# Layer 1 of a two-layer graph transformer: the squares of the first normalization a chunk behind their sums, and the turn of h behind the products of the next to last formed pair

## The chip, the core and the metric

The kernel runs on one core of one Trainium2 chip. A core has five engines that each work through a queue of their own, in order, and wait for one another at semaphores: TensorE (PE in the profile; its weight loads are PEld), VectorE (DVE), ScalarE (ACT), GpSimd (POOL) and SyncE (SP, which here only issues DMAs). POOL issues the indirect DMAs, too: gathers that fetch listed rows, and puts that store rows at listed places. The metric is the device time of one execution in microseconds, and the kernel before takes 1840.38 us in the median of three runs.

## The reference

Two layers of the same form follow each other on 2708 tokens of width 512, with 8 heads of 64 and a hidden width of 2048. Each token attends to the tokens that a sparse 0/1 matrix names (its own included), and then passes a feed-forward part. Everything is float32.

```python
q, k, v = (h @ Wq.T + bq), (h @ Wk.T + bk), (h @ Wv.T + bv)        # 8 heads of 64
scores = where(mask == 0, -1e9, einsum('nhd,mhd->hnm', q, k) / 8)
ctx = einsum('hnm,mhd->nhd', softmax(scores), v).reshape(n, 512)
h1 = layer_norm(h + ctx @ Wo.T + bo, ln1_g, ln1_b)                 # the first normalization
h2 = layer_norm(h1 + relu(h1 @ W1.T + b1) @ W2.T + b2, ln2_g, ln2_b)
```

## The kernel before, in words

**Work by edges.** Attention is done over the listed neighbours alone. The 2708 tokens are sorted by their number of neighbours into 22 tiles of 128 (the last has 20), and each tile has a fixed number of places for neighbours. Two places make a *step*: POOL gathers the two rows of keys and values (`kv`, L1119, one gather a place), DVE multiplies the keys by the queries (L1156), adds up the scores (L1162), and, for a step begun three steps earlier, weights the first row of values (L1192) and adds both to the sum (L1199). ACT takes the exponentials of a step begun two steps earlier (`p`, L1175) and weights its second row of values, a head at a time (L1182, eight instructions). When a tile's steps are over, DVE makes the sums of its weights (L1207 to L1222) and ACT divides (`cx`, L1230, eight instructions). A gather reuses the place of an earlier step's rows, and so waits for that step's L1199.

**Blocks and chunks.** The projections, normalizations and the feed-forward part are done for blocks of two tiles (256 tokens), numbered k = 0 to 10 here. The feed-forward part of a block runs over 16 chunks f of 128 hidden units: PE makes the chunk's hidden values (`pf`, L1601 or L1785, four products), ACT adds a bias and cuts at zero (`ft`, L1796 in the formed blocks). In blocks 0, 1 and 10, two more products for each chunk add to the block's output (`second`, L1574), three chunks behind. In layer 1's blocks 2 to 9, the *formed* blocks (`feed_forward_by_seven`), two chunks make a pair, and the eight products of a pair are replaced by seven half-width ones (`products(j)`, L1774) on sums that DVE forms (`sums(j)`, L1751 to L1754); the last pair is done plainly (L1805, L1809) between `products(5)` and `products(6)`.

**What runs beside a block.** While block k is in its feed-forward part, the next block is made ready by the generator `attended`: PE turns `cx` (`tp`, L1354; the copy back is ACT's `cT`, L1359) and multiplies by Wo (`o`, L626); DVE adds the residual and makes the sum over the row in one instruction (`total`, L1312, `h<-o,xb`; the negated mean `nm` follows, L1323); ACT makes the sum of squares (`squares`, L1329); POOL makes the reciprocal root from it (`centred`, `va` L1336 and `rd` L1338) and DVE subtracts the mean and multiplies by the gain (L1339); ACT scales (`scaled`, L1345, `h<-h,rd`). Then PE turns `h` (`turned`: eight `tp<-ident,h`) and ACT copies it to `hT` (L1359, eight instructions), which all 16 chunks of the next block read. `hT` has one buffer. The block before, k-1, is finished by the generator `ended` (the *tail*): squares, centred, scaled, then POOL adds the shift by an accumulating DMA (L1348, `h<-ln_b`) and puts the rows to the output (L1082, `out<-h`). An `h` buffer (four of them) is written again by `total` two blocks later, once its put has landed.

**What sets the order.** The order is written out by hand for all five engines: the loop at the end of `by_edges` walks over the chunks of each block, and at each chunk takes the next piece of `attended`, of the tail and of the attention. The tail's pieces go by the table `TAILS` (the first entry up to block 2, the second for later blocks); attention goes by credits in the tables `PACES` (block 0), `PACE` and `PACE7` (the formed blocks), which `advance` turns into whole steps. In layer 1 the pieces of `attended` stand at chunks 10 to 13, the turn at chunk 15 ahead of that chunk's `advance`. Each `yield` in a generator is a place where the loop puts in other work; what stands behind a waiting instruction on its engine waits with it.

Of the kernel before, what the change touches and what calls it, by code (L numbers as in the profile page):

```python
# [25 lines left out]
NFC = FF // P  # L26
# [29 lines left out]
    (0.0,) * 4 + (0.6,) + (1.3,) * 4 + (0.6,) * 2 + (0.0,) * 2 + (0.5, 0.8, 2.4),  # L56
    (0.0,) * 4 + (0.4, 1.1, 0.3, 1.1, 0.3, 1.0, 1.0, 1.5, 0.4, 0.9, 0.0, 2.2),
)
TAILS = ((1, 2, 4, 5, 8), (5, 7, 8, 9, 10))
FORMED = (1, 1)  # L60
FORMS = (3, 5, 7, 9, 11, 13, 15)
PACE = (
# [425 lines left out]
def by_edges(ctx: ExitStack, tc: tile.TileContext, x, xT, adj, layers, out, redo):  # L488
# [874 lines left out]
    class Layer:  # L1363
# [132 lines left out]
        def attended(self, block, got, xbs=None, soon=False):  # L1496

            cTs, hs, norms = [], [], []

            def turn(g):  # L1500
                r = size(g)
                cx = got.pop(g)
                cT = dn.tile([P, NC, P], F32, tag="cT", name="cT", bufs=3)
                flip(cx, r, cT[:, :, :r], self.bv)
                cTs.append((g, r, cT))

            turn(block[0])
            xbs = xbs or self.residuals(block)
            yield
            if block == blocks[0]:  # L1510
                turn(block[1])
                yield
            for i, xb in enumerate(xbs):
                g, r, cT = cTs[i]
                o = project(lambda c: cT[:, c, :r], r, self.wo, "o")
                h = dn.tile([P, DM], F32, tag="h", name="h", bufs=4)
                if self.n == 0 or soon:
                    nc.vector.tensor_tensor(h[:r], o[:r], xb[:r], ALU.add)
                    plus_rest(h[:r], o, r)
                    if self.n == 0:  # L1520
                        nc.vector.tensor_tensor(h[:r], h[:r], self.bo[:r], ALU.add)
                    norm(h, r, self.g1, None if soon else self.e1b2)
                else:
                    last = xb[:r]
                    parts = [o[:r]] + rest(o, r)
                    for part in parts[:-1]:
                        nc.vector.tensor_tensor(h[:r], part, last, ALU.add)
                        last = h[:r]
                    norms.append(Norm(h, r, self.g1, xb).total(parts[-1], last))
                hs.append(h)  # L1530
                if len(cTs) == 1:
                    turn(block[1])
                for one in norms[-1:]:
                    one.squares()
                yield
            if norms:
                for one in norms:
                    one.centred()
                yield
                for one in norms:  # L1540
                    one.scaled()
            yield hs
# [10 lines left out]
        def feed_forward(self, block, hs, hT):  # L1553
# [70 lines left out]
            if apart:  # L1624
                for f in range(4):
                    second(f, block[1], slice(0, DM // 2))
                quarters(NFC - 1)
            for g in () if apart else block:
                for f in range(NFC - LAG, NFC):
                    second(f, g)  # L1630
                    if g == block[-1] and f == NFC - LAG:
                        quarters(NFC - 1)
# [106 lines left out]
        def feed_forward_by_seven(self, k, block, hs, hT):  # L1739
# [41 lines left out]
            for f in range(NFC):  # L1781
                j = f // 2
                pf = ps_f.tile([P, DM], F32, tag="f", name="pf")
                for c in range(NC):
                    nc.tensor.matmul(  # L1785
                        pf[:, :W],
                        self.w1[j][:, c, f % 2 * P : f % 2 * P + P],
                        hT[:, c, :],
                        start=(c == 0),
                        stop=(c == NC - 1),  # L1790
                    )
                if f % 6 < 4:
                    ft = dn.tile([P, W], F32, tag="ft", name="ft", bufs=4)
                else:
                    ft = self.more_fts[f % 2]
                nc.scalar.activation(ft, pf[:, :W], AF.Relu, bias=self.b1[:, f : f + 1])  # L1796
                fts.append(ft)
                if f % 2 == 0 and j > 0:
                    sums(j - 1)
                yield None  # L1800
                if f % 2 and j > 1:
                    products(j - 2)
            for i in range(2):
                f, w = 2 * J + i, self.w2[J]
                nc.tensor.matmul(a0, fts[f][:, :P], w[:, i, :], start=False, stop=False)  # L1805
# [248 lines left out]
    for n in range(NL):  # L2054
# [48 lines left out]
        for k, block in enumerate(blocks):  # L2103
# [12 lines left out]
            else:  # L2116
                working = now.feed_forward(block, hs, hT)
            for f, zs in enumerate(working):
                if f == NFC:
                    break  # L2120
                if n > 0 and f == 2:
                    for g, h in zip(block, hs):
                        added_row(h, size(g), now.e1b2)
# [11 lines left out]
                if more and f == 11 + 2 * (k + n == 0):  # L2135
                    until(blocks[k + 1][1])
                    next(projecting)
                if more and n > 0 and f in (12, 13):
                    next(projecting)
                if more and n == 0 and f == 12 + 2 * (k == 0):  # L2140
                    *_, hs_next = projecting
                if more and f == NFC - 1:
                    finish(asking)
                    hT = now.turned(blocks[k + 1], hs_next)
                advance((PACE7 if seven else PACE if k else PACES)[n][f])
                if more and n > 0 and f == 13:
                    *_, hs_next = projecting
                if f in (0, 3, 7, 9) and (f or k):
                    next(asking, None)
                if k == 0 and len(now.w1) < NFC // 2 and f % 2 == 0:  # L2150
# [132 lines left out]
```

## Time and profile before

| | us |
|---|---|
| three runs: median (lowest to highest) | 1840.38 (1840.02 to 1844.04) |
| the profiled execution's own time | 1839.64 |
| its span, first to last instruction | 1837.4 |
| PE busy in the span | 1793.4 (98%) |
| DVE busy | 1484.5 (81%) |
| ACT busy | 1000.9 (54%) |
| POOL busy | 852.1 (46%) |

Layer 1's feed-forward part begins at 1142.79 us of the span (block 0) and its last block at 1791.80 us. Starts and lengths are in microseconds from the first instruction; in a waits row the columns are the waiting engine, its tile and line, what it waited for, then the total, the number of waits and the longest. In a timeline row they are start, length, engine, line, operation, what it writes and reads, and the number of instructions merged into the row; the bracket at the end is the idle time ahead of it and what ended it. A windows row gives a stretch, its length, and for each engine the busy time in it, then the granted clock of TensorE as a share. Ends of matmuls are modelled, so starts are the safer reading. An engine's idle time is put down to what came last before it ended.

### The profile page before, as it was taken

Reading aid. Unit: us, or ns where it says so; the run is one execution under the profiler, and the core shown is the slowest. Engines: PE = TensorE matmul, PEld = TensorE weight load, DVE = VectorE, ACT = ScalarE, POOL = GpSimd, SP = SyncE. Lnnn points to the kernel's source line nnn. Section 1 sums busy time; section 2 is a strip of 40 time slices with the busy share of each in tenths; the row PEclk is TensorE's granted clock in tenths of the full one; section 3 lists DMA queues with packets and bytes.
Section 4 is the critical chain, followed back from the end, with each engine's and each line's share of the span. In section 5 each row is a group of like instructions: output and inputs, shape, how many; then the busy total and the mean of one; then the engine's idle time right before and its main releaser. Section 6 shows DMA issues by size and latency. Waiting matters only on the chain. (4 is left out here: it accounts for less than half of the span.)

```text
span 1837.4 us, 24293 instructions
## 1 busy us (share of the span) xinstructions
PE 1793.4 (98%) x6931; PEld 1233.9 (67%) x6931; DVE 1484.5 (81%) x2667; ACT 1000.9 (54%) x3399; POOL 852.1 (46%) x830
## 2 busy tenths in 40 slices
PE   9999999999999999999999999999999999999997
PEld 4444456567776867777777545666887788778776
DVE  5986778988989888899885277888988989889953
ACT  4770445554556546475553114677665767577641
POOL 3234755544445544454430133466555555555512
PEclk9999999999999999999999999999999999999999
DMA  9997987756676666666652877967787887876731
GB/s 342 374 338 257 371 279 238 243 177 222 209 240 229 205 218 205 224 231 187 222 185 83 301 279 255 318 193 280 235 256 227 278 256 218 275 222 191 225 86 35
DMA packets 192777, 432.26 MB, mean 235 GB/s; under 512 B 21222, under 2 KB 89946, under 8 KB 192632
## 3 DMA queue, kind: packets, MB, share of 16 engines
q0 software_dynamic: 76992, 264.49, 44.3%
q1 hardware_dynamic: 105482, 144.51, 23.1%
q10 hardware_dynamic: 10158, 21.61, 3.1%
q8 instruction: 57, 0.93, 0.2%
q14 instruction: 88, 0.72, 0.1%
HBM read 362.63 MB, written 57.11 MB: 228 GB/s over the span
## 5 line engine op out<-in xcount | busy, mean ns | idle before, releaser
L1119 POOL DMA_INDIRECT kv<-kv_d,listed x420 | 521.1, 1241 | 442.1 <-DVE acc L1199 172.5
L1785 PE MATMUL pf<-hT,w 128*128 128x256 f32 x2048 | 467.1, 380 | 9.1 <-ACT ft L1796 9.1
L1785 PEld LDWEIGHTS pf<-hT,w 128*128 128x128 f32 x2048 | 387.6, 190 | 75.2 <-ACT ft L1796 12.2
L1182 ACT ACTIVATE kv<-kv,p 128x64 f32<-128x64 f32 x1232 | 311.0, 334 | 5.0
L1156 DVE TENSOR_TENSOR kv<-kv,q 128x1024 f32<-128x1024 f32 (+1 forms) x222 | 256.9, 1157 | 17.3 <-DMA q<-q_d,ident_i 10.8
L1162 DVE TENSOR_REDUCE sc<-kv 128x16 f32<-128x1024 f32 (+1 forms) x222 | 258.0, 1162 | 7.6
L1199 DVE TENSOR_TENSOR acc<-acc,kv 128x1024 f32<-128x1024 f32 (+2 forms) x178 | 205.5, 1155 | 37.1 <-ACT kv L1182 23.1
L1796 ACT ACTIVATE ft<-pf,b 128x256 f32<-128x256 f32 x192 | 88.7, 466 | 232.8 <-PE pf L1785 218.2
L1175 ACT ACTIVATE p<-sc,listed 128x8 f32<-128x8 f32 x420 | 103.4, 295 | 106.9 <-DVE sc L1162 85.4
L1601 PEld LDWEIGHTS pf<-hT,w 128*128 128x128 f32 x768 | 130.2, 190 | 39.4 <-issue 24.9
L1601 PE MATMUL pf<-hT,w 128*128 128x256 f32 (+1 forms) x768 | 155.1, 350 | 0.1
L626 PE MATMUL o<-wo,cT 128*128 128x512 f32 x336 | 151.2, 594 | 2.5 <-ACT cT L1359 1.8
L1286 POOL TENSOR_TENSOR rd<-va,mhalf 128x1 f32<-128x1 f32 (+1 forms) x48 | 43.8, 912 | 224.7 <-DVE va L1284 224.2
L1574 PE MATMUL a<-w,ft 128*128 128x512 f32 x288 | 135.1, 593 | 0.0
L1192 DVE TENSOR_TENSOR kv<-kv,p 128x512 f32<-128x512 f32 (+1 forms) x178 | 123.8, 695 | 3.4 <-ACT p L1175 3.2
L626 PEld LDWEIGHTS o<-wo,cT 128*128 128x128 f32 x336 | 63.2, 190 | 70.8 <-issue 60.1
L751 DVE MAX8 tops<-code 128x8 f32<-128x247 f32 (+2 forms) x242 | 78.6, 400 | 27.2 <-ACT code L746 27.0
L1230 ACT ACTIVATE cx<-acc,su 128x64 f32<-128x64 f32 (+1 forms) x352 | 88.3, 335 | 14.4 <-DVE su L1222 11.9
L1182 ACT ACTIVATE acc<-kv,p 128x64 f32<-128x64 f32 (+1 forms) x352 | 88.8, 334 | 1.4
L1774 PE MATMUL a<-w,forms 128*128 128x256 f32 x288 | 85.7, 379 | 0.0
L1774 PE MATMUL c<-w,forms 128*128 128x256 f32 x288 | 85.7, 379 | 0.0
L746 ACT ACTIVATE code<-aj 128x1354 bf16<-128x1354 int32 (+1 forms) x44 | 73.4, 1722 | 20.5 <-POOL aj L740 16.6
(258 smaller groups left out, 2820.3 us busy)
## 6 DMA issues: line engine op xcount, KB each, us to landing
forms<-form_d SPq DMA_DIRECT2D x336, 128.0 KB
aj<-in_adj SPq DMA_DIRECT2D x42, 677.0 KB
kv_d<-kvs ACTq DMA_DIRECT2D x21, 512.0 KB
h<-ln_b POOLq DMA_DIRECT2D x41, 256.0 KB
xg<-in_xT SPq DMA_DIRECT2D x19, 512.0 KB
w<-in_W SPq DMA_DIRECT2D x16, 512.0 KB
kv<-kv_d,listed POOLq DMA_INDIRECT x420
zT_d<-zT SPq DMA_DIRECT2D x22, 256.0 KB
```

The lines of the kernel that those rows point to most:

```text
L626: nc.tensor.matmul(o[:r], xs(c), wm[:, c, :], start=(c == 0), stop=(c == NC - 1))
L1119: return nc.gpsimd.indirect_dma_start(out=to, out_offset=None, in_=table[:, :], in_offset=bass.IndirectOffsetOnAxis(ap=s, axis=0), bounds_ ...
L1156: nc.vector.tensor_tensor(kv[:r, :c, :DM], kv[:r, :c, :DM], self.q[:r].unsqueeze(1).to_broadcast([r, c, DM]), ALU.mult,)
L1162: nc.vector.tensor_reduce(self.sc[:r, s0 : s0 + c, :], kv[:r, :c, :DM].rearrange("p s (h d) -> p s h d", d=DK), AX.X, ALU.add,)
L1175: nc.scalar.activation(p[:r, s, :], self.sc[:r, s, :], AF.Exp, bias=minus[:r, g, s : s + 1])
L1182: nc.scalar.activation(to[:, i, hd], kv[:r, i, DM + h * DK : DM + (h + 1) * DK], AF.Copy, scale=p[:r, s0 + i, h : h + 1],)
L1192: nc.vector.tensor_tensor(to[:, 0, :].rearrange("p (h d) -> p h d", d=DK), kv[:r, 0, DM:].rearrange("p (h d) -> p h d", d=DK), p[:r, s0, : ...
L1199: nc.vector.tensor_tensor(self.acc[:r, :c, :], self.acc[:r, :c, :], kv[:r, :c, DM:], ALU.add)
L1574: nc.tensor.matmul(a[:r, cols], fts[f][:, c0 : c0 + r], self.w2[f // 2][:, f % 2, cols], start=(f == 0), stop=(f == NFC - 1),)
L1601: nc.tensor.matmul(pf[:, :w], self.w1[f // 2][:, c, f % 2 * P : f % 2 * P + P], hT[:, c, :w], start=(c == 0), stop=(c == NC - 1),)
L1774: nc.tensor.matmul(to, left, right, start=start, stop=stop)
L1785: nc.tensor.matmul(pf[:, :W], self.w1[j][:, c, f % 2 * P : f % 2 * P + P], hT[:, c, :], start=(c == 0), stop=(c == NC - 1),)
```

## The change

Five places change, all of them in the order of layer 1; the instructions are the same ones.

1. In `attended`, the squares of a tile are issued one chunk behind its `total`, so at chunks 12 and 13 instead of 11 and 12; `centred` moves to chunk 14 and `scaled` to chunk 15.
2. The loop turns `h` where the generator of the feed-forward part yields once more, behind its 16 chunks: in the formed blocks this stands behind `products(5)`, ahead of the last pair; in blocks 0 and 1 behind the last products of the block's first tile.
3. Chunk 15's `advance`, which stood behind the turn, now stands ahead of it.
4. The second entry of `TAILS` is one lower throughout: the tails from block 3 on are issued a chunk earlier.
5. The end of the loop is told by a list of outputs instead of by the chunk's number.

```diff
-TAILS = ((1, 2, 4, 5, 8), (5, 7, 8, 9, 10))
+TAILS = ((1, 2, 4, 5, 8), (4, 6, 7, 8, 9))
...
             for i, xb in enumerate(xbs):
+                for one in norms:
+                    one.squares()
                 g, r, cT = cTs[i]
...
-                for one in norms[-1:]:
-                    one.squares()
                 yield
             if norms:
+                norms[-1].squares()
+                yield
                 for one in norms:
                     one.centred()
                 yield
...
             for g in () if apart else block:
+                if self.n == NL - 1 and g == block[-1]:
+                    yield None
                 for f in range(NFC - LAG, NFC):
                     second(f, g)
...
                 if f % 2 and j > 1:
                     products(j - 2)
+            if self.n == NL - 1:
+                yield None
             for i in range(2):
...
             for f, zs in enumerate(working):
+                if zs:
+                    break
                 if f == NFC:
-                    break
+                    hT = now.turned(blocks[k + 1], hs_next)
+                    continue
...
-                if more and n > 0 and f in (12, 13):
+                if more and n > 0 and f in (12, 13, 14):
                     next(projecting)
+                if more and n > 0 and f == NFC - 1:
+                    *_, hs_next = projecting
...
                 if more and f == NFC - 1:
                     finish(asking)
-                    hT = now.turned(blocks[k + 1], hs_next)
+                    if n == 0:
+                        hT = now.turned(blocks[k + 1], hs_next)
                 advance((PACE7 if seven else PACE if k else PACES)[n][f])
-                if more and n > 0 and f == 13:
-                    *_, hs_next = projecting
```

**The end of block 5, PE.** Before, the turn of `h` follows the products of chunks 14 and 15 (`pf`):

```order
L1785 MATMUL pf<-hT,w_8330 128x256 x8
L1354 MATMUL tp<-ident,h 128x128 x8
L1774 MATMUL a_11896<-forms 128x256
L1774 MATMUL c_11818<-forms 128x256
L1774 MATMUL c_11819<-forms 128x256
L1774 MATMUL c_11818<-w_8305,forms 128x256
L1774 MATMUL a_11895<-w_8305,forms 128x256
L1774 MATMUL c_11819<-w_8305,forms 128x256
L1774 MATMUL a_11895<-w_8305,forms 128x256
L1805 MATMUL a_11895<-w_8920,ft 128x512 x2
```

Now:

```order
L1789 MATMUL pf<-hT,w_8330 128x256 x8
L1778 MATMUL a_11896<-forms 128x256
L1778 MATMUL c_11818<-forms 128x256
L1778 MATMUL c_11819<-forms 128x256
L1778 MATMUL c_11818<-w_8305,forms 128x256
L1778 MATMUL a_11895<-w_8305,forms 128x256
L1778 MATMUL c_11819<-w_8305,forms 128x256
L1778 MATMUL a_11895<-w_8305,forms 128x256
L1354 MATMUL tp<-ident,h 128x128 x8
L1811 MATMUL a_11895<-w_8920,ft 128x512 x2
```

The turn has moved behind the seven products of pair 5; the last pair (L1805, L1809) and `products(6)` are what is left between it and the next block.

**The end of block 5, ACT.** Before, `u` (L1827) is the copy of a sum of the block that has just ended:

```order
L1345 ACTIVATE h<-h,rd 128x512 x2
L1796 ACTIVATE ft<-pf,b_8175 128x256 x2
L1359 ACTIVATE hT<-tp,ln_b 128x128 x8
L1175 ACTIVATE p<-sc,listed 128x8 x2
L1182 ACTIVATE kv<-kv,p 128x64 x8
L1230 ACTIVATE cx<-acc,su 128x64 x8
L1175 ACTIVATE p<-sc,listed 128x8 x2
L1182 ACTIVATE kv<-kv,p 128x64 x8
L1827 COPY u_12385<-c_11818 128x256
```

Now:

```order
L1800 ACTIVATE ft<-pf,b_8175 128x256 x2
L1345 ACTIVATE h<-h,rd 128x512 x2
L1175 ACTIVATE p<-sc,listed 128x8 x2
L1182 ACTIVATE kv<-kv,p 128x64 x8
L1230 ACTIVATE cx<-acc,su 128x64 x8
L1175 ACTIVATE p<-sc,listed 128x8 x2
L1182 ACTIVATE kv<-kv,p 128x64 x8
L1359 ACTIVATE hT<-tp,ln_b 128x128 x8
L1833 COPY u_12385<-c_11818 128x256
```

The scaling stands behind both evictions of `ft`, and the attention of chunk 15 (two steps, and here the division of a tile) stands between the scaling and the copies to `hT`.

**The end of block 7, DVE**, from the second tile's `total` on. Before:

```order
L1312 ISA h,zsum<-o,xb 128x512
L1312 ISA zsum 128x1
L1323 TENSOR_SCALAR nm<-zsum 128x1
L1339 SCALAR_TENSOR_TENSOR h<-h,nm,ln_g 128x512 x2
L1156 TENSOR_TENSOR kv<-kv,q 128x2x512
L1162 TENSOR_REDUCE sc<-kv 128x16
L1192 TENSOR_TENSOR kv<-kv,p 128x512
L1199 TENSOR_TENSOR acc<-acc,kv 128x1024
L1751 TENSOR_TENSOR forms<-ft 128x128
L1752 TENSOR_TENSOR ft<-ft 128x128
```

Now:

```order
L1312 ISA h,zsum<-o,xb 128x512
L1312 ISA zsum 128x1
L1323 TENSOR_SCALAR nm<-zsum 128x1
L1156 TENSOR_TENSOR kv<-kv,q 128x2x512
L1162 TENSOR_REDUCE sc<-kv 128x16
L1192 TENSOR_TENSOR kv<-kv,p 128x512
L1199 TENSOR_TENSOR acc<-acc,kv 128x1024
L1755 TENSOR_TENSOR forms<-ft 128x128
L1756 TENSOR_TENSOR ft<-ft 128x128
L1757 TENSOR_TENSOR forms<-forms,ft 128x128
L1758 TENSOR_TENSOR forms<-ft,forms 128x128
L1339 SCALAR_TENSOR_TENSOR h<-h,nm,ln_g 128x512 x2
```

A step of attention and the four sums of a pair have moved ahead of `centred` (L1339).

**Block 5, POOL**, from the shift for the block's own residual (the first `h<-ln_b`) to the tail's put. Before:

```order
L1348 DMA h<-ln_b 128x512 x2
L1119 DMA kv<-kv_d_112,listed 128x1024 x4
L1336 TENSOR_SCALAR va<-sq 128x1
L1338 TENSOR_TENSOR rd<-va,mhalf 128x1
L1336 TENSOR_SCALAR va<-sq 128x1
L1338 TENSOR_TENSOR rd<-va,mhalf 128x1
L1119 DMA kv<-kv_d_112,listed 128x1024 x2
L1348 DMA h<-ln_b 128x512 x2
L1119 DMA kv<-kv_d_112,listed 128x1024 x2
L1082 DMA out<-h,ident_i 2708x512 x2
```

Now:

```order
L1348 DMA h<-ln_b 128x512 x2
L1119 DMA kv<-kv_d_112,listed 128x1024 x2
L1336 TENSOR_SCALAR va<-sq 128x1
L1338 TENSOR_TENSOR rd<-va,mhalf 128x1
L1336 TENSOR_SCALAR va<-sq 128x1
L1338 TENSOR_TENSOR rd<-va,mhalf 128x1
L1119 DMA kv<-kv_d_112,listed 128x1024 x4
L1348 DMA h<-ln_b 128x512 x2
L1082 DMA out<-h,ident_i 2708x512 x2
```

The tail's roots stand two gathers earlier; the tail's shift (the second `h<-ln_b`) still has six gathers between it and the first, and the put follows it at once. In blocks 6, 7 and 8 this number stays what it was (five, six and eight); in blocks 3 and 4 it falls from seven to five and from eight to six.

## The prediction

> **What bounds the kernel now.** The page comes first:
>
> ```profile
> PE 1793.4 (98%) x6931; PEld 1233.9 (67%) x6931; DVE 1484.5 (81%) x2667; ACT 1000.9 (54%) x3399; POOL 852.1 (46%) x830
> ```
>
> TensorE has 44 us of idle time in the whole span, so a reordering can win little, and everything it can win lies in PE's waits. Those stand in the view of waits, asked for PE and ACT:
>
> ```profile
> PE tp L1354 <- ACT h L1345: 9.4, 8, 2.4
> PE pf L1785 <- ACT ft L1796: 9.1, 7, 2.6
> ACT xb L1329 <- DVE nm L1323: 48.9, 13, 6.9
> ```
>
> The first row is the turn waiting for the scaled `h` (9.4 us in 8 waits). The second is PE waiting for an eviction of the formed blocks; the third says why ACT is late there: it stands at the squares, waiting for DVE's mean, with `ft` queued behind. These two are what the change is aimed at. Where they fall is read from the windows, one for each block of layer 1, from the block's first `pf` to the next block's (columns: PE, PEld, DVE, ACT, POOL busy, granted clock, DMA share, GB/s); the last row is a short piece behind the turn in block 6:
>
> ```profile
> 1214.16:1277.87 63.71, 63.71 (x225) 41.13 (x224) 56.07 (x76) 49.43 (x183) 44.44 (x41) 1.00 0.82 277
> ...
> 1339.30:1405.62 66.32, 61.77 (x271) 49.60 (x270) 58.52 (x100) 42.50 (x153) 36.34 (x35) 1.00 0.75 236
> 1405.62:1472.08 66.46, 63.09 (x272) 50.67 (x271) 59.25 (x99) 44.77 (x162) 35.67 (x35) 0.97 0.82 258
> 1472.08:1535.11 63.03, 61.69 (x271) 49.60 (x270) 57.00 (x96) 44.82 (x161) 34.88 (x34) 1.00 0.81 251
> 1535.11:1600.40 65.29, 62.88 (x271) 50.94 (x270) 58.63 (x101) 40.95 (x144) 40.88 (x39) 0.97 0.81 246
> 1600.40:1665.47 65.07, 61.75 (x272) 49.61 (x271) 56.30 (x92) 44.49 (x161) 34.19 (x31) 1.00 0.68 211
> 1665.47:1728.55 63.08, 61.52 (x271) 49.60 (x270) 58.16 (x104) 44.48 (x161) 38.87 (x36) 1.00 0.78 243
> ...
> 1588.90:1592.00 3.10, 3.10 (x10) 2.65 (x11) 3.07 (x4) 3.07 (x13) 0.67 (x1) 0.50 0.84 244
> ```
>
> Block 1 is the first row, then come blocks 3 to 8; block 2 is the stretch between them, 61.43 us. A formed block's own PE work is about 61.7 us, so idle time is 4.55 in block 3, 3.37 in block 4, 1.34, 2.41, 3.32 and 1.56 in blocks 5 to 8 (length less PE). DVE has 57 to 59 us of work in 63 to 66 us: it is the engine that is next, and a thing ordered later on DVE is really later.
>
> **How late `h` is, and what follows it.** The end of block 5 on PE (the turn, the start of the last pair, the next block's first product):
>
> ```profile
> 1524.51 1.27 PE L1354 MATMUL tp<-ident,h 128*128 128x128 f32 x8 [1.05 <-ACT h L1345]
> ...
> 1528.64 1.88 PE L1805 MATMUL a<-w,ft 128*128 128x512 f32 x4
> ...
> 1535.11 1.24 PE L1785 MATMUL pf<-hT,w 128*128 128x256 f32 x5
> ```
>
> Last pair and `products(6)` take 1535.11 − 1528.64 = 6.47 us; that is what covers the copies to `hT` now. On ACT, the same place:
>
> ```profile
> 1525.69 2.14 ACT L1359 ACTIVATE hT<-tp,ln_b 128x128 f32<-128x128 f32 x8
> 1527.69 0.52 ACT L1175 ACTIVATE p<-sc,listed 128x8 f32<-128x8 f32 x2
> ...
> 1530.21 2.02 ACT L1230 ACTIVATE cx<-acc,su 128x64 f32<-128x64 f32 x8
> ...
> 1534.57 0.35 ACT L1827 COPY u<-c 128x256 f32<-128x256 f32 x1
> ```
>
> The eight copies take 2.00 us (to 1527.69). The attention of chunk 15 takes 6.88 us (1527.69 to 1534.57), of which a step is 2.52 (to 1530.21), so two steps without the division of a tile take 5.04. Today it follows the copies; in the change it precedes them. The orders show it with the division in blocks 1 to 5 and as two bare steps in blocks 0, 6, 7 and 8.
>
> On DVE, the second tile's `total` of blocks 2 to 8, with what follows it in block 7, and the pair of `centred` in block 5 (1.41 us):
>
> ```profile
> 1322.92 0.68 DVE L1312 CUSTOM_DVE_ANT_0 h<-o,xb 128x512 f32<-128x512 f32 x1
> 1389.83 0.69 DVE L1312 CUSTOM_DVE_ANT_0 h<-o,xb 128x512 f32<-128x512 f32 x1
> 1453.37 0.69 DVE L1312 CUSTOM_DVE_ANT_0 h<-o,xb 128x512 f32<-128x512 f32 x1
> 1516.89 0.69 DVE L1312 CUSTOM_DVE_ANT_0 h<-o,xb 128x512 f32<-128x512 f32 x1
> ...
> 1522.03 1.41 DVE L1339 SCALAR_TENSOR_TENSOR h<-h,nm,ln_g 128x512 f32<-128x512 f32 x2
> ...
> 1581.43 0.69 DVE L1312 CUSTOM_DVE_ANT_0 h<-o,xb 128x512 f32<-128x512 f32 x1
> 1649.68 0.69 DVE L1312 CUSTOM_DVE_ANT_0 h<-o,xb 128x512 f32<-128x512 f32 x1
> ...
> 1650.48 0.74 DVE L1339 SCALAR_TENSOR_TENSOR h<-h,nm,ln_g 128x512 f32<-128x512 f32 x1
> ...
> 1652.12 1.22 DVE L1156 TENSOR_TENSOR kv<-kv,q 128x1024 f32<-128x1024 f32 x1
> ...
> 1656.36 0.28 DVE L1751 TENSOR_TENSOR forms<-ft 128x128 f32<-128x128 f32 x1
> ...
> 1712.76 0.69 DVE L1312 CUSTOM_DVE_ANT_0 h<-o,xb 128x512 f32<-128x512 f32 x1
> ```
>
> From `total` to the next instruction are 0.80 us (1649.68 to 1650.48), a step is 4.24 (1652.12 to 1656.36), four sums are 4 × 0.28 = 1.13 with their gaps. So in the new order the second scaled tile is finished at `total` + 0.80 + 4.24 + 1.13 + 1.41 + 0.80 (the scaling, 0.72, and its hand-over) = `total` + 8.38.
>
> **The formed blocks, term by term.** From the scaling two things lead to the next block. PE: half the turn 0.6, then 6.47, together 7.07. ACT: the attention of chunk 15, then five of the eight copies, 5/8 × 2.00 = 1.25, since the first product needs the first piece of both tiles: 6.88 + 1.25 = 8.13 with the division, 5.04 + 1.25 = 6.29 without. The later decides: 8.13 in blocks 2 to 5, 7.07 in blocks 6 to 8. With one step between `total` and `centred` the next block starts at `total` + 16.51 or + 15.45; blocks 4 and 5 have two steps there, so + 20.75. Against the starts in the windows:
>
> Block 2: 1322.92 + 16.51 = 1339.43, now 1339.30: +0.1. Block 6: 1581.43 + 15.45 = 1596.88, now 1600.40: −3.5. Block 7: 1665.13 against 1665.47, and block 8: 1728.21 against 1728.55: −0.35 each. In blocks 3 to 5, a wait for the tail's put (its buffer is written again by the first tile's `total`) comes in:
>
> ```profile
> 1379.14 0.69 DVE L1312 CUSTOM_DVE_ANT_0 h<-o,xb 128x512 f32<-128x512 f32 x1 [1.97 <-DMA out<-h,ident_i]
> 1446.94 0.69 DVE L1312 CUSTOM_DVE_ANT_0 h<-o,xb 128x512 f32<-128x512 f32 x1 [2.72 <-DMA out<-h,ident_i]
> 1510.53 0.69 DVE L1312 CUSTOM_DVE_ANT_0 h<-o,xb 128x512 f32<-128x512 f32 x1 [3.30 <-DMA out<-h,ident_i]
> ```
>
> The earlier tails take a pair of gathers from in front of the put in blocks 3 and 4, so I let 1.97 and 2.72 go: block 3 is 1389.83 − 1.97 + 16.51 = 1404.37 against 1405.62, −1.25; block 4 is 1453.37 − 2.72 + 20.75 = 1471.40 against 1472.08, −0.7. In block 5 the number of gathers ahead of the put is unchanged, so the 3.30 stays: 1516.89 + 20.75 = 1537.64 against 1535.11, +2.5; if the put landed in time after all, −0.8. Together blocks 2 to 8: −3.55. The gains from the squares (ACT no longer stands in front of `ft`) are in this sum already, since PE's way to the turn gets shorter while `h` decides when the turn may start.
>
> **Blocks 0 and 1.** Here only the last tile's products, 2.6 us, stand behind the new turn, and the roots on POOL have moved behind a further pair of gathers:
>
> ```profile
> 1194.96 0.69 DVE L1312 CUSTOM_DVE_ANT_0 h<-o,xb 128x512 f32<-128x512 f32 x1 [5.81 <-PE o L626]
> ...
> 1202.48 1.25 POOL L1119 DMA_INDIRECT kv<-kv_d,listed  x1 [11.57 <-issue]
> ...
> 1205.11 1.03 POOL L1336 TENSOR_SCALAR va<-sq 128x1 f32<-128x1 f32 x1
> ...
> 1207.74 0.72 ACT L1345 ACTIVATE h<-h,rd 128x512 f32<-128x512 f32 x1 [0.19 <-POOL rd L1338]
> ...
> 1270.33 0.47 ACT L1612 ACTIVATE ft<-pf,b 128x256 f32<-128x256 f32 x1
> ```
>
> A pair of gathers holds POOL 2.63 us (1202.48 to 1205.11); from the first root to the scaled second tile are 1207.74 + 0.72 − 1205.11 = 3.35. Block 0, if the added pair waits for DVE's second step as other gathers do: that step ends at 1194.96 + 0.80 + 4.24 + 1.41 + 4.24 = 1205.65, the pair starts some 0.75 behind it (an estimate, after the 0.80 from `total` to its follower), `h` is scaled at 1206.4 + 2.63 + 3.35 = 1212.4, and 6.29 later, at 1218.7, block 1 begins: +4.5 on 1214.16. If the pair finds its place free, the first pair starts 1.64 earlier (`centred` is no longer ahead of its step) and the roots 2.63 later: about +1.6. I take +4.5: a gather reuses the place of an earlier step, and POOL's 11.57 us of idle time ahead of the pair at 1202.48 show it waiting here, not lagging. Block 1: `h` is scaled behind the last `ft`, at 1270.33 + 0.47 + 2 × 0.72 = 1272.2, and 8.13 later is 1280.4 against 1277.87: +2.5; the bounds are 0 (the copies overtaken by nothing but one step) and +2.5. Sum of everything: 7.0 − 3.55 = +3.45.
>
> **The clock.** The granted clock was 0.50 for 3.1 us in block 6, behind the 2.4 us wait of its turn, and the 0.97 of blocks 4 and 6 says the same; such a dip loses 1.55 us. Of blocks 3 to 8, four had over 2 us of idle time (3, 4, 6 and 7), and two of the four a dip. With my terms over 2 us stand in blocks 0, 1, 3, 4, 5 and 7, the longest above 3: I count three dips in six, one more than now, +1.6 (bounds 0 and four more, +6). Total +5.0.
>
> The Trainium skill (TensorE: Matmul & The Clock Gate, What's actually happening) puts the clock's fall behind an idle window of about 3.4 us. This trace shows a fall behind 2.4 us, so the measurement decides; by the rule alone only the gaps of blocks 0 and 5 would bring one, as many as the two shown now, and the sum would stay at +3.45.
>
> **The edits that cost nothing.** The tail's ACT and DVE pieces a chunk earlier are covered by the 20 us in which ACT is idle in each block; without that cover they would cost 2 to 3 us a block at the first `ft`. Squares a chunk later are covered by the step that follows `total` on DVE.
>
> **Sum.** The profiled execution took 1839.64; +5.0 gives 1844.6, and the median of the three runs is 0.7 above that execution: **1845.4**.
>
> **Rivals.** *B, gains and losses meet:* block 0's pair finds its place (+1.6 instead of +4.5), block 5's put lands in time (−0.8 instead of +2.5), no further dip: 5.0 − 2.9 − 3.3 − 1.6 = −2.8, so 1838. For it: both are a matter of 3 us; against: POOL's 11.57 us of idle time above, and the unchanged number of gathers ahead of block 5's put. *C, the turn stops being waited for:* in blocks 3 to 8 PE loses no time, 16.5 us less (the idle times above), with blocks 0 and 1 as forecast, +7: 1830. For it: three more microseconds of products ahead of the turn exceed every single tp wait (2.4 at most). Against: `centred` moves back by 5.4 us (step and sums) at the same time, more than the turn does. *D, the put holds POOL:* slower by more. The tail's put now follows its accumulating shift at once:
>
> ```profile
> 1495.31 1.92 POOL L1348 DMA_DIRECT2D h<-ln_b  x2
> ...
> 1502.79 1.02 POOL L1082 DMA_INDIRECT out<-h,ident_i  x1 [1.48 <-DMA h<-ln_b]
> ```
>
> The shift landed 7.5 us after its issue, so POOL stands up to 5.6 us instead of 1.48, with the gathers queued behind. If DVE has under 4 us of gathered rows in store there, it waits for keys, 4.1 us in each of blocks 5 to 8 at most: up to +16, half of it likelier, so about 1854.
>
> **How the numbers follow.** Forecast (a net loss of 2 to 10) 0.45, its own range 1838 to 1850; B 0.27; C 0.17; D 0.11. The likeliest alone gives 1845.4. The range reaches from C's middle with the clock undisturbed, 1828, to D's, 1854. A measurement tells some 0.2%, 3.7 us, from no change. Faster by more: C and a fifth of B, 0.22; slower by more: two thirds of the forecast and D, 0.41; within: 0.37.
>
> **What would show it.** Right: a wait of PE's `tp` for `h` of about 3 us in block 5; the first `pf` of blocks 2 to 6 waiting for copies to `hT` that stand behind `cx`; block 1 starting 4 us later; the put's wait of `total` gone in blocks 3 and 4 and there in block 5. C would show as cycles of 61 to 62 us in blocks 5 to 8, D as DVE waiting for `kv` behind `out<-h`. I am wrong if DVE reaches the second `total` several microseconds earlier than now, since each later time hangs on it.

## The result, and the profile after

The change takes 1847.88 us in the median of 20 runs, the kernel before 1844.22 in 20 runs beside them: a ratio of 1.0020, 95% interval 1.0011 to 1.0030, so about 4 us slower. The forecast was 1845.4 against 1840.38, 5 us slower. The two profiled executions are further apart, 1846.97 against 1839.64: the profiled one of the kernel before lies 4.6 us under its median of 20. So single blocks are compared here by their own length and the whole by the ratios, and a sum of block lengths overstates the loss.

The windows of the changed kernel, one a block of layer 1, blocks 0 to 9 (columns as before: length, then PE, PEld, DVE, ACT, POOL busy, granted clock):

```profile
1141.13:1216.42 75.29, 70.63 (x241) 43.00 (x239) 60.37 (x78) 44.09 (x165) 34.39 (x31) 0.98 0.75 249
1216.42:1282.49 66.07, 63.98 (x225) 41.05 (x225) 56.09 (x72) 50.97 (x190) 44.89 (x43) 1.00 0.85 277
1282.49:1345.12 62.63, 62.63 (x270) 50.96 (x271) 51.79 (x90) 40.27 (x143) 30.50 (x33) 0.97 0.75 231
1345.12:1409.56 64.44, 61.79 (x271) 49.58 (x271) 58.60 (x100) 42.84 (x154) 33.45 (x35) 1.00 0.79 248
1409.56:1476.10 66.54, 63.11 (x270) 50.86 (x271) 61.25 (x100) 45.68 (x165) 39.79 (x37) 0.97 0.80 258
1476.10:1539.52 63.42, 61.45 (x272) 49.58 (x270) 57.64 (x96) 44.61 (x161) 36.96 (x35) 1.00 0.81 250
1539.52:1601.02 61.50, 61.17 (x270) 49.88 (x271) 56.09 (x96) 41.73 (x148) 33.26 (x34) 1.00 0.77 246
1601.02:1667.03 66.01, 62.88 (x271) 50.63 (x270) 58.34 (x95) 44.83 (x162) 32.81 (x34) 0.97 0.72 218
1667.03:1735.45 68.42, 63.03 (x271) 50.98 (x270) 58.51 (x104) 44.77 (x161) 36.39 (x36) 0.95 0.74 229
1735.45:1799.12 63.67, 61.13 (x271) 49.33 (x270) 37.75 (x78) 30.36 (x103) 10.44 (x15) 0.97 0.36 92
```

| block | 0 | 1 | 2 | 3 | 4 | 5 | 6 | 7 | 8 |
|---|---|---|---|---|---|---|---|---|---|
| before, us | 71.37 | 63.71 | 61.43 | 66.32 | 66.46 | 63.03 | 65.29 | 65.07 | 63.08 |
| change, us | 75.29 | 66.07 | 62.63 | 64.44 | 66.54 | 63.42 | 61.50 | 66.01 | 68.42 |
| difference | +3.9 | +2.4 | +1.2 | −1.9 | +0.1 | +0.4 | −3.8 | +0.9 | +5.3 |
| forecast | +4.5 | +2.5 | +0.1 | −1.25 | −0.7 | +2.5 | −3.5 | −0.35 | −0.35 |

Blocks 0, 1, 3 and 6 came out as forecast; block 8 is the surprise, 5.7 us above its forecast, and block 5 lies 2.1 us below its own. Together the nine blocks are 8.5 us longer, and 6.4 us in a second profiled execution of the change (below), against 3.45 forecast for them without the clock and 5.0 with it. PE's waits of the changed kernel (total, times, longest):

```profile
PE tp L1354 <- ACT h L1345: 16.8, 8, 5.4
PE pf L1789 <- ACT hT L1359: 3.9, 3, 2.1
...
PE pf L1789 <- ACT ft L1800: 1.6, 2, 0.8
PE pf L1603 <- ACT hT L1359: 1.2, 1, 1.2
```

The waits for `ft` fell from 9.1 to 1.6 us: the later squares do what they are for. But the waits for the scaled `h` rose from 9.4 to 16.8, and 5.1 us of waits for `hT` are new. On DVE, two rows of the kernel before, and the same two of the change:

```profile
DVE h L1312 <- DMA out<-h,ident_i: 13.8, 6, 3.3
...
DVE kv L1156 <- DMA kv<-kv_d,listed: 6.2, 4, 3.4
```

```profile
DVE kv L1156 <- DMA kv<-kv_d,listed: 11.6, 8, 3.2
...
DVE h L1312 <- DMA out<-h,ident_i: 2.0, 2, 1.7
```

DVE hardly waits for the tail's put any more, except in block 8 (1.70 us, 1.06 before), but it waits for gathered keys instead. Where that happens is seen in block 8, in three timelines of the change. POOL:

```profile
1691.91 1.91 POOL L1348 DMA_DIRECT2D h<-ln_b  x2
1701.78 1.74 POOL L1082 DMA_INDIRECT out<-h,ident_i  x1 [7.96 <-DMA h<-ln_b]
```

DVE:

```profile
1705.54 0.69 DVE L1312 CUSTOM_DVE_ANT_0 h<-o,xb 128x512 f32<-128x512 f32 x1 [1.70 <-DMA out<-h,ident_i]
...
1712.66 1.24 DVE L1156 TENSOR_TENSOR kv<-kv,q 128x1024 f32<-128x1024 f32 x1 [3.17 <-DMA kv<-kv_d,listed]
...
1718.23 0.69 DVE L1312 CUSTOM_DVE_ANT_0 h<-o,xb 128x512 f32<-128x512 f32 x1
...
1724.58 1.41 DVE L1339 SCALAR_TENSOR_TENSOR h<-h,nm,ln_g 128x512 f32<-128x512 f32 x2
```

PE:

```profile
1726.18 1.97 PE L1354 MATMUL tp<-ident,h 128*128 128x128 f32 x8 [5.38 <-ACT h L1345]
```

The put stands 7.96 us at POOL for the shift just ahead of it to land; the gathers queued behind come late, DVE stands 3.17 us for their keys, the second `total` is 3.9 us later in the block than before, and `centred` stands a step and four sums behind that. PE then waits 5.38 us.

### The profile page after: what moved, and what is told of

The parts are those of the page before. It is cut to its first block, busy times and chain, and to the rows that moved or that the text cites. A ratio compares the mean times of both kernels' runs of the same rounds, so it can differ in the third digit from the quotient of the medians.

```text
span 1844.6 us, 24300 instructions
## 1 busy us (share of the span) xinstructions
PE 1798.3 (97%) x6931; PEld 1237.2 (67%) x6931; DVE 1486.1 (81%) x2667; ACT 1002.6 (54%) x3399; POOL 838.9 (45%) x830
## 5 line engine op out<-in xcount | busy, mean ns | idle before, releaser
L626 PEld LDWEIGHTS o<-wo,cT 128*128 128x128 f32 x336 | 63.4, 190 | 69.3 <-issue 57.6
```

The source lines that it names most:

```text
L626: nc.tensor.matmul(o[:r], xs(c), wm[:, c, :], start=(c == 0), stop=(c == NC - 1))
```

## The experiments

Each ratio is to the kernel before on the same chip, with its 95% interval. 0.1% is 1.8 us. L-numbers are each kernel's own. "Layer 1" below is the length of blocks 0 to 9 together in the profiled execution: 649.0 us before and 658.0 in the change.

**The attention of chunk 15 behind the turn.**

```diff
                 if f == NFC:
                     hT = now.turned(blocks[k + 1], hs_next)
+                    advance((PACE7 if seven else PACE if k else PACES)[n][NFC - 1])
                     continue
...
-                advance((PACE7 if seven else PACE if k else PACES)[n][f])
+                if not (more and n > 0 and f == NFC - 1):
+                    advance((PACE7 if seven else PACE if k else PACES)[n][f])
```

> The change with one difference: the attention of chunk 15 is issued behind the turn instead of ahead of it, so on ACT the eight copies to hT come first. Theory (the copies are late because they stand behind attention): the waits of pf for hT (5.1 us in four places in the changed kernel) go, DVE's order and the tp waits (16.8 us) stay, and the time falls by about 4 to 5 us against the change, to about the kernel before. Rival (the attention is only pushed on, and u and the first ft of the next block become late): the 5 us come back as pf or forms waiting for ft or u, and the time stays at the change's, 0.2% above the kernel before.

1.0011 (0.9998 to 1.0023), median 1844.66. The row of `pf` waiting for `hT` is gone from the list, tp waits are 13.6 us, and layer 1 is 648.5 us, but 4.5 us of waits for `ft` came back (longest 2.9, early in block 2). The ratio lies under the change's by 0.1%, inside its interval: that the copies were late behind the attention is shown, that it costs 5 us is not. The profiled execution, 1837.25 us, is the fastest of the twelve, so its 648.5 overstates the gain. Its blocks 0 and 1 take 72.7 and 63.7 us (75.3 and 66.1 in the change, 71.4 and 63.7 before), while block 2, where `ft` is now late, takes 65.4 instead of 62.6.

**The old normalization with the new turn.**

```diff
-                for one in norms:
-                    one.squares()
...
+                for one in norms[-1:]:
+                    one.squares()
                 yield
             if norms:
-                norms[-1].squares()
-                yield
                 for one in norms:
                     one.centred()
...
-                if more and n > 0 and f in (12, 13, 14):
+                if more and n > 0 and f in (12, 13):
                     next(projecting)
-                if more and n > 0 and f == NFC - 1:
-                    *_, hs_next = projecting
...
                 advance((PACE7 if seven else PACE if k else PACES)[n][f])
+                if more and n > 0 and f == 13:
+                    *_, hs_next = projecting
```

> The change with the first normalization at its old chunks (squares right behind total, centred at chunk 13, scaled behind it); the turn behind the products of pair 5, the attention ahead of the copies and the tails stay as changed. Theory (the turn alone is the gain, the later normalization is the loss): tp waits for h fall from 16.8 to under 3 us, pf waits for ft come back to about 9 us (the squares stand in front of ft again), and the time falls 4 to 9 us below the change, 1 to 5 us below the kernel before. Rival (the later squares pay): the 7.5 us of ft waits that the change removed come back and nothing else goes, so the time rises by about 3 to 7 us above the change.

0.9946 (0.9929 to 0.9964), median 1833.96, 14 us below the change's ratio and more than I expected. PE's waits there:

```profile
PE pf L1792 <- ACT ft L1803: 7.9, 6, 3.1
PE pf L1792 <- ACT hT L1359: 3.5, 3, 1.9
```

No wait of the turn for `h` is left in the list; the waits for `ft` are back, as both sides expected, and it pays all the same. The later normalization costs more than the squares' place wins.

**The old tails.**

```diff
-TAILS = ((1, 2, 4, 5, 8), (4, 6, 7, 8, 9))
+TAILS = ((1, 2, 4, 5, 8), (5, 7, 8, 9, 10))
```

> The change with the tails at their old chunks (5, 7, 8, 9, 10). Theory (the earlier put frees the buffer of h for the first total, but its wait for the shift's landing holds POOL's gathers): the waits of total for the put return to 10 us or more, the waits of kv for gathers fall from 11.6 to about 6 us; the blocks 3 to 5 get 2 to 3 us longer, blocks 7 and 8 stay or get shorter, and the time changes by -3 to +3 us against the change. Rival (the put alone cost the blocks 7 and 8): the time falls by 5 us or more, tp waits of blocks 7 and 8 (3.1 and 5.4 us) go down to 1 us.

1.0064 (1.0044 to 1.0083), median 1856.18. The waits moved as the theory said:

```profile
DVE h L1312 <- DMA out<-h,ident_i: 16.4, 6, 3.7
...
DVE kv L1156 <- DMA kv<-kv_d,listed: 4.8, 6, 2.0
```

but the time did not stay within 3 us: 8 us above the change. Block 8 takes 65.5 us there against 68.4, block 7 65.0 against 66.0, while blocks 3 to 5 take 68.5, 69.0 and 67.2 against 64.4, 66.5 and 63.4. Both mechanisms are there; the gain of the put's earlier landing is much the larger.

**Blocks 0 and 1 as before**, the change in blocks 2 to 9 alone:

```diff
-                if more and n > 0 and f in (12, 13, 14):
+                if more and n > 0 and f in ((12, 13, 14) if seven else (12, 13)):
                     next(projecting)
...
-                    if n == 0:
+                    if n == 0 or not (seven):
                         hT = now.turned(blocks[k + 1], hs_next)
```

(with the squares, the scaling and the second yield made to depend on `seven` likewise)

> The change in the formed blocks 2 to 9 alone: blocks 0 and 1 have the old normalization, the old turn and the old place of the attention. Theory (blocks 0 and 1 lose 3.9 and 2.4 us in the profiles): they come back to 71.4 and 63.7 us, and the time falls by about 6 us against the change, to 2 or 3 us under the kernel before. Rival (the loss of the two blocks only reappears later, since DVE's attention is what is late): the time stays within 2 us of the change.

0.9983 (0.9970 to 0.9997), median 1839.60; blocks 0 and 1 take 71.37 and 63.71 us again. So their loss in the change, 6.3 us in the profiles and 7 us by the ratios, is a loss of the whole, and comes back nowhere.

**The new tails alone**, on the kernel before (the edit of the table, reversed from above):

> The kernel before with the new tails (4, 6, 7, 8, 9) and nothing else of the change. Theory (the tails are a gain of their own, since the put frees the buffer of h before the first total wants it): the waits of total for the put fall from 13.8 us to under 4, the waits of kv for gathers rise from 6.2 to about 11 us, and the time falls 4 to 8 us below the kernel before (with the old tails in the changed kernel it was 8 us longer). Rival (the tails pay only with the late turn): the time stays within 2 us of the kernel before.

0.9939 (0.9922 to 0.9956), median 1833.75, 11 us below the kernel before. The waits for the put are 1.8 us, those for keys 9.5:

```profile
DVE kv L1156 <- DMA kv<-kv_d,listed: 9.5, 5, 3.3
DVE h L1312 <- DMA out<-h,ident_i: 1.8, 2, 1.0
```

So one line of the diff is worth more than twice what the whole change loses.

**The old turn with all else changed.**

```diff
                 if f == NFC:
-                    hT = now.turned(blocks[k + 1], hs_next)
                     continue
...
-                    if n == 0:
-                        hT = now.turned(blocks[k + 1], hs_next)
+                    hT = now.turned(blocks[k + 1], hs_next)
```

> The change with the old turn: the later squares and the new tails stay, but h is turned at chunk 15 ahead of its attention, in all blocks. Theory (the later normalization makes h late by a step and a set of sums, 5.4 us, and the moved turn only gives 3 us of it back): tp waits for h rise from 16.8 to about 35 us, pf waits for hT go, and the time is 8 to 20 us above the change. Rival (the attention ahead of the copies is the main loss): the time falls below the change.

1.0126 (1.0104 to 1.0148), median 1868.08, with

```profile
PE tp L1354 <- ACT h L1345: 36.8, 10, 6.6
```

against an expected 35. The later normalization on top of the tails costs 1.87%, 34 us; the moved turn takes 20 of them back. It wins where `h` is late, and the change makes it late.

**The turn moved in blocks 2 to 9 alone**, old normalization, the attention behind the turn, new tails (the edits above together):

> The moved turn in the formed blocks alone, with the normalization at its old chunks, the new tails, and the attention of chunk 15 behind the turn; blocks 0 and 1 as before. Theory: blocks 0 and 1 take 71.4 and 63.7 us again (2.7 less than with the early normalization in all blocks), the waits of pf for hT (3.5 us there) go too, tp waits stay away, and the time is 3 to 6 us below that run, 13 to 16 us below the kernel before. Rival (with the attention behind the copies ft of the next block is late instead): 2 to 3 us below that run only.

0.9921 (0.9903 to 0.9939), median 1831.62; layer 1 is 637.4 us, with the tails alone 639.6. The waits for `hT` went, those for `ft` stayed at 8.6. It lies 5 us below the run with the old normalization, as expected, and 3 us below the tails alone; in both cases the intervals overlap.

**The same with the shift a chunk earlier and the put two behind it.**

```diff
-TAILS = ((1, 2, 4, 5, 8), (4, 6, 7, 8, 9))
+TAILS = ((1, 2, 4, 5, 8), (3, 5, 6, 7, 9))
```

> The run before this one (moved turn in the formed blocks, old normalization, copies first) with the tail's shift a chunk earlier still and the put two chunks behind it: (3, 5, 6, 7, 9) instead of (4, 6, 7, 8, 9). Theory (the put holds POOL's gathers because it stands right behind the shift that it waits for): with gathers between them POOL waits under 4 us at the put instead of 6 to 8, the waits of kv for gathers in blocks 7 and 8 (2.7 and 2.4 us) go, and the time falls by 2 to 5 us more. Rival (the gathers are late for another reason, the DMA queues' load): the waits of kv stay, and the time is within 1.5 us of that run.

0.9878 (0.9858 to 0.9897), median 1824.02: 22 us faster than the kernel before, the fastest of all, and 8 us below the run before this one, more than the 2 to 5 expected. Block 8's POOL, with gathers between shift and put:

```profile
1671.79 1.90 POOL L1348 DMA_DIRECT2D h<-ln_b  x2 [2.52 <-ACT h L1345]
1673.99 1.64 POOL L1119 DMA_INDIRECT kv<-kv_d,listed  x1 [0.30 <-issue]
...
1680.84 1.06 POOL L1082 DMA_INDIRECT out<-h,ident_i  x1 [0.30 <-issue]
```

and its blocks 5 to 8, in which PE never stops:

```profile
1470.17:1531.01 60.84, 60.84 (x271) 49.87 (x270) 58.41 (x98) 44.71 (x163) 35.01 (x35) 1.00 0.84 264
1531.01:1591.86 60.85, 60.85 (x272) 49.87 (x271) 58.39 (x99) 42.55 (x154) 37.40 (x37) 1.00 0.81 254
1591.86:1652.70 60.84, 60.84 (x272) 49.87 (x271) 56.22 (x93) 44.57 (x162) 37.13 (x34) 1.00 0.78 237
1652.70:1713.54 60.84, 60.84 (x272) 49.87 (x270) 57.86 (x104) 44.66 (x162) 38.90 (x36) 1.00 0.76 248
```

In blocks 5 to 8 POOL stands at most 3.0 us ahead of the put, and DVE has no wait for keys over 0.3 us there. The put that stood behind its own shift was the cause of the late keys; that the shift is also issued a chunk earlier belongs to the same edit and isn't priced apart.

**The kernel before with these tails.**

> The kernel before with the tails at (3, 5, 6, 7, 9), put two chunks behind the shift, and nothing of the change. Theory (the tail sets when DVE can run on, the turn's place matters little once DVE is early): waits of total for the put and the mid-block waits of kv for gathers both stay under 4 us, blocks 5 to 8 take 61 to 63 us, and the time is 12 to 18 us below the kernel before; the moved turn with the same tails was 21 us below. Rival (the moved turn makes most of that): 11 us below, as with the tails (4, 6, 7, 8, 9).

0.9893 (0.9878 to 0.9909), median 1827.05, about 20 us faster than before, a little more than expected. The moved turn's 0.15% on top is within the intervals; in the profiles it is 4 us (layer 1 634.4 against 630.3), PE still waiting 6.6 us for `h` here.

**The whole change with these tails.**

> The whole change with the tails at (3, 5, 6, 7, 9) instead of (4, 6, 7, 8, 9). Theory (the later normalization costs by itself, also where POOL holds up nothing): the waits of kv for gathers fall from 11.6 to about 4 us, block 8 comes down from 68.4 to 63 to 65 us, tp waits stay over 10 us, and the time is 4 to 8 us below the change, still 14 us or more above the moved turn with the old normalization and these tails. Rival (the later normalization lost only because POOL's put came at the wrong time): within 5 us of that run.

0.9947 (0.9933 to 0.9961), median 1837.04, 13 us below the change, more than expected, and 13 us above the fastest. Block 8 fell to 61.8 us and the waits for keys to 4.3, so the put's hold cost the change more than I had put on it. The waits of the turn for `h` are 7.6 us, not over 10. Still the later normalization and the new turn together lose 0.54%, 10 us, to the kernel before with the same tails: blocks 0, 1 and 2 take 74.8, 66.1 and 62.6 us, and block 4 66.6. Blocks 6 to 8 take 61.0, 61.1 and 61.8, 1.3 us together above the 60.84 each of the fastest run: there the change had lost by the put's hold, and what it still loses lies in the earlier blocks.

**The gaps filled, and the change once more beside it.**

```diff
         tp = ps.tile([P, NC, P], F32, tag="g", name="tp")
+        for _ in range(fill):
+            nc.tensor.matmul(tp[:, 0, :], ones, ident, start=True, stop=True)
...
                 if f == NFC:
-                    hT = now.turned(blocks[k + 1], hs_next)
+                    hT = now.turned(blocks[k + 1], hs_next, 16 * (k in (0, 4, 7, 8)))
```

> The change with 16 extra 128x128 products (of the identity with ones, overwritten unread by the turn) ahead of the turn of blocks 0, 4, 7 and 8, about 2.1 us of work that fills most of PE's wait for h there (3.2, 2.6, 3.1 and 5.4 us in the changed kernel's profile). h comes no earlier. Theory (an idle gap of over 2 us costs a stretch of half clock behind it, 1.55 us each): the gaps shrink to under 1.5 us in blocks 0, 4 and 7, their half-clock stretches go, and the time falls by 3 to 6 us against the change. Rival (the half clock hides in waits that would be there anyway): the time is within 1 us of the change. If the fillers delay the turn the time rises by up to 2 us a block.

> The change itself once more, beside the run with the filled gaps, so that both stand on the same chip: 0.1 to 0.3% above the kernel before, PE waiting 14 to 20 us for h at the turn in layer 1, with a half clock behind some of the longer waits.

The filled kernel: 1.0001 (0.9990 to 1.0012), median 1847.06; the change beside it: 1.0015 (1.0003 to 1.0026), median 1848.68. The intervals overlap; by the ratios it is 2.6 us, by the medians 1.6, less than the 3 to 6 expected. The 16 products took 3.6 us, not 2.1. The clock did come back: blocks 4, 7 and 8 of the filled kernel, then of the change beside it:

```profile
1413.25:1479.41 66.16, 64.94 (x302) 53.32 (x302) 61.23 (x100) 45.27 (x163) 38.71 (x37) 1.00 0.81 257
...
1604.19:1670.18 65.99, 64.85 (x304) 53.50 (x302) 56.80 (x93) 44.53 (x162) 33.16 (x33) 1.00 0.70 218
1670.18:1736.44 66.26, 64.85 (x303) 53.50 (x302) 58.24 (x104) 44.64 (x162) 38.49 (x36) 1.00 0.76 234
```

```profile
1410.69:1477.33 66.64, 63.20 (x270) 50.65 (x271) 61.25 (x100) 45.77 (x165) 39.35 (x37) 0.97 0.80 258
...
1602.72:1668.34 65.62, 62.95 (x271) 50.62 (x270) 58.27 (x95) 44.96 (x162) 33.14 (x34) 0.97 0.73 220
1668.34:1736.66 68.32, 63.10 (x271) 51.05 (x270) 58.46 (x104) 44.77 (x161) 39.52 (x36) 0.95 0.73 230
```

Block 8 won 2.1 us, block 4 only 0.5, block 7 nothing. The last is no sign of a hidden half clock. In block 7 DVE waited 2.1 us longer for keys in the filled kernel (first row) than in the change beside it (second row); that wait ends 8.6 us ahead of the block's fillers:

```profile
1649.09 1.22 DVE L1156 TENSOR_TENSOR kv<-kv,q 128x1024 f32<-128x1024 f32 x1 [4.61 <-DMA kv<-kv_d,listed]
```

```profile
1645.57 1.23 DVE L1156 TENSOR_TENSOR kv<-kv,q 128x1024 f32<-128x1024 f32 x1 [2.49 <-DMA kv<-kv_d,listed]
```

From the last scaled tile to the next block the fillers saved 1.7 us in block 7 (8.69 to 7.02) and 1.8 in block 8 (8.82 to 7.01), but 0.4 in block 4 (8.55 to 8.11) and nothing in block 0 (6.18 in both). In blocks 0 and 4, PE's slow products run beside the copies to `hT`, which in block 4 start only behind 6.8 us of attention: the half clock is hidden there. Where PE's own work decides the end, it counts in full.

## Why the prediction was right, and where not

The sign, the size and the paths behind `total` held; the account of POOL did not, in two steps that erred against each other. That the loss came out within 1.4 us of the forecast is therefore partly luck.

**Blocks 0 and 1** (+4.5, +2.5): right in size and cause. In block 0 the added pair of gathers waits for DVE's second step, as chosen:

```profile
1204.46 0.99 POOL L1119 DMA_INDIRECT kv<-kv_d,listed  x1 [2.59 <-DVE acc L1199]
1205.76 0.99 POOL L1119 DMA_INDIRECT kv<-kv_d,listed  x1 [0.30 <-issue]
1206.83 1.09 POOL L1336 TENSOR_SCALAR va<-sq 128x1 f32<-128x1 f32 x1
```

Undoing the two blocks took the whole 7 us away. The pair holds `h` up, as forecast; the run with the copies ahead of the attention shows that the attention in front of them has its share in both blocks.

**`total` + 8.38, and the later of two ways from there**: right. In block 8, `centred` starts 6.35 us behind `total` (1718.23 to 1724.58), 6.17 by the sum. The end of block 5 in the change, ACT and then PE:

```profile
1530.03 1.39 ACT L1345 ACTIVATE h<-h,rd 128x512 f32<-128x512 f32 x2 [2.77 <-DVE h L1339]
...
1538.10 2.13 ACT L1359 ACTIVATE hT<-tp,ln_b 128x128 f32<-128x128 f32 x8
```

```profile
1530.81 1.32 PE L1354 MATMUL tp<-ident,h 128*128 128x128 f32 x8 [1.04 <-ACT h L1345]
...
1539.52 1.78 PE L1789 MATMUL pf<-hT,w 128*128 128x256 f32 x7 [0.92 <-ACT hT L1359]
```

From the scaled tiles (1530.03 + 1.39 = 1531.42) to the next block are 8.1 us, 8.13 in the forecast, and it is the copies that decide. From the second `total` to the next block, blocks 2 to 8 take 16.1, 16.1, 21.3, 20.9, 15.8, 17.1 and 17.2 us, against 16.5, 16.5, 20.75, 20.75 and three times 15.45. Only blocks 7 and 8 are clearly longer, by 1.7 and 1.8: the half clock behind the turn's wait, which the filled kernel saves there.

**"In block 5 the number of gathers ahead of the put is unchanged, so the 3.30 stays": wrong, and with it the size of the tails.** What is unchanged in block 5 is the number ahead of the *shift*, six. Ahead of the put there were eight, and in the change there are six: the pair between shift and put is gone, as the orders above show. The put and the first `total` behind it, in block 5 of the change:

```profile
1506.94 2.12 POOL L1082 DMA_INDIRECT out<-h,ident_i  x1 [5.58 <-DMA h<-ln_b]
```

```profile
1511.56 0.69 DVE L1312 CUSTOM_DVE_ANT_0 h<-o,xb 128x512 f32<-128x512 f32 x1 [0.26 <-DMA out<-h,ident_i]
```

The put starts no earlier than before: 30.8 us into the block (1506.94 − 1476.10), 30.7 before (1502.79 − 1472.08), for it still waits for the shift. But `total`, which waits for its landing, now starts 4.6 us behind it, before 7.7 (1510.53 − 1502.79). The runs that differ by the tails alone agree: 7.1 us in the change with the old tails, 4.8 in the kernel before with the new ones. So the 3.30 went, as rival B had it for this block. In blocks 3 and 4 the put does start earlier, by 9.0 and 6.8 us into the block.

The waits for the put fell from 13.8 us to 2.0 in all, where I had let 1.97 and 2.72 go. Blocks 6 to 8 had such waits too (1.58, 3.17 and 1.06 us), and the forecast left them out. The sign named for being wrong appeared: the second `total` of blocks 3 to 5 comes 2.2, 2.5 and 2.3 us earlier in its block, the last of them uncounted. Alone, the tails are worth 11 us.

**Rival D was real, in blocks 7 and 8, beside the forecast and not instead of it.** The put behind its own shift held POOL 6.2 us in block 7 and 8.0 in block 8, more than the 5.6 of the rival, and DVE waited 3.17 us for keys in block 8 (above) and 2.64 in block 7:

```profile
1644.29 1.23 DVE L1156 TENSOR_TENSOR kv<-kv,q 128x1024 f32<-128x1024 f32 x1 [2.64 <-DMA kv<-kv_d,listed]
```

Block 8's −0.35 became +5.3 by it: 3.9 us of that are the later second `total`, the rest mostly the half clock behind the turn's wait. In blocks 5 and 6 the same order held POOL 5.6 and 3.4 us, and DVE had no key wait over 0.8 us there. I had put the rival at 0.11, as a fate of the whole change, where it was a term of the sum.

**The price of the later normalization was counted per block through waits, and is larger**: 14 us with the new turn (1.0020 against 0.9946), 34 with the old one. The forecast never took it by itself: it stood against the starts of a kernel that waited for its puts, and a part of the tails' gain was thus booked as a smaller loss. How much of the 14 us is the later `h` itself isn't told apart: with the put moved away from its shift, the change costs 1.3 us in blocks 6 to 8 together.

**The clock**: I counted one more dip at 1.55 us. The change has three more (blocks 0, 2, 7 and 8 show one that they did not have, block 6 has lost its own); in its second profiled execution block 2 has none. Filling four of its gaps won about 2 us. The number was too low. The price was about right where PE decides the block's end (1.7 and 1.8 us in blocks 7 and 8) and too high where the copies do (0 and 0.4 us in blocks 0 and 4).

## What to carry to other kernels

Price a change's parts apart, the one-line table too: here the tail's issue times were worth 11 us, and 20 with the put moved away from its shift, while the edits that fill the diff lost 15 (1.0020 against 0.9939). An indirect DMA that waited for another DMA's landing held the gathers behind it on POOL, here for 3 to 8 us in blocks 5 to 8, so put work that doesn't depend on it in between. And moving a consumer later pays only as far as its producer is late: the moved turn won 20 us where `h` was late, and 3 us, within the intervals, where it was not. Before moving the turn behind more products, see whether `h` can be made early.

## What the runs showed of the hardware

**The clock falls behind shorter gaps than expected, and not always.** Over the layer-1 parts of all 14 profiled executions, each idle gap of PE over 1 us (ends of matmuls are modelled) is set beside the granted clock in the 4 us behind it: gaps under 1.78 us were followed by a half clock 0 times in 31, from 1.78 to 2.65 us 23 times in 40, from 2.65 to 4 us 16 times in 20, above 4 us 9 times in 9. The same gap can go either way: block 2 begins behind a gap of 2.08 us in the change and of 2.09 in its second run, and its first 3 us are, in the one and the other:

```profile
1282.49:1285.49 3.00, 3.00 (x8) 2.44 (x9) 1.48 (x6) 0.72 (x3) 0.83 (x1) 0.57 0.82 227
```

```profile
1285.40:1288.40 3.00, 3.00 (x14) 2.66 (x15) 1.48 (x6) 1.19 (x4) 0.84 (x1) 1.00 0.95 270
```

The block took 62.63 us with the dip and 60.95 without: 1.68 us, beside the 1.55 that the forecast used and the 1.7 and 1.8 saved in blocks 7 and 8. The Trainium skill (TensorE: Matmul & The Clock Gate, What's actually happening) puts the fall behind an idle window of about 3.4 us, free-running: that it depends on more than the gap agrees with these runs, that it takes 3.4 us does not.

**A product cost twice a turn of the same shape.** In block 4 of the filled kernel the 16 filling products of 128x128 appear as 32 instructions and took 3.57 us from their start to the next start, 0.22 a product; the eight turns behind them appear as eight and took 0.88 us, 0.11 each. The estimate of 2.1 us for the fillers had priced a product like a turn.
